# A recurrent kernel on one core: the opening's loads in another order, the cell ahead of long sums, the head's work dealt anew

## The chip, the cores and the metric

One core of a Trainium2 chip runs the kernel. Its engines are the tensor engine (PE, with its weight loads shown as PEld), the vector engine (DVE), the scalar engine (ACT), GpSimd (POOL), and SyncE (SP), whose queue issues every DMA of this kernel. The 16 DMA engines of the core serve that one queue. The metric is the time of one execution on the device in microseconds (us), as the median of several runs; lower is better.

## The reference

The kernel computes an LSTM over 512 steps for a batch of 32, hidden size 512, and adds the result to its input, all in float32:

```python
xW = einsum('ntd,dg->ntg', x, Wx) + b        # (32, 512, 2048)
def step((h, c), xw_t):
    a = xw_t + h @ Wh                         # four gates of 512
    i, f, o = sigmoid(a[:, :512]), sigmoid(a[:, 512:1024]), sigmoid(a[:, 1024:1536])
    g = tanh(a[:, 1536:])
    c = f * c + i * g
    h = o * tanh(c)
    return (h, c), h
out = x + hs                                  # hs: the h of all steps
```

## The kernel before, in words

**Two kinds of matmul.** Each of the 512 steps needs the recurrent product `h @ Wh` (`h_part`, L254), which depends on the step before, and the projection `x @ Wx` of its own x. The projection of steps 20 to 499 is not made step by step. It is made for 15 groups of 32 steps with a scheme of Strassen's kind: 26 products per group, each as seven small products `r` (L541), between left factors made of sums of rows of x (`pair_sum` L486 to L492, `make_sum` L455, held in `xs0`, `xs1` and `ubuf`) and right factors made of sums of weight blocks. Each product ends in a C buffer (`evacuate`, L595 to L611), and the C buffers are combined with long sums of 128x1024 (`w_op`, L402) and stored to DRAM (`xwd`), from where each step's four gate rows are read back three steps ahead (`load_xw`). This work is called the stream. It is counted in quarters: four to a small product, 28 to a product, 728 to a group. The first group's stream lies in the head, steps 0 to 19. Later groups are dealt evenly over the steps.

**Opening and head.** Before step 0, PE makes plain projections for steps 0 to 4 (`KEPT`) and for step 13 (`FIRST`), L190. The projections of steps 5 to 12 and 14 to 19 are made inside the head steps, as `HEAD_PLAINS` deals them; those of steps 11 and later wait in `xw` or in DRAM (`kept`). `HEAD_STREAM` says how many quarters each head step takes. In the same time DVE makes the sums of weight blocks: 8 to 25 by `v_sum` (L711 for whole tiles, L714 for three pieces), in rooms that are reused in the order of `V_ROOMS`, and SP stores them to `vdram` (L718, two DMAs of 768 and 128 KB each), from where each row of the stream loads its right factors into a ring of three (`vring`, `load_v`). A room is overwritten only when its store has landed. Eight of the factors are raw weight blocks (`v_raw`, `V_DIRECT`). `jobs[t]` says what of this falls into step t, behind which projection.

**The order inside a head step.** `h_part(t)` is issued first, then the stores and loads of the step's top on SP. What follows is a list of chunks: a plain projection, or some quarters of the stream. From a given step on the first chunk is 24 quarters. In a stream chunk the program issues in this order: loads of right factors, u sums, `evacuate`, pair sums that are due (`row_jobs`), more u sums, long sums while the planner's account `room["dve"]` of free DVE time allows it, bias copies into the banks (`seed_banks`, L574; eleven products start from a combination of bias rows), the matmuls, and, behind the first chunk, the cell (`cell`, L269 to L288). Every engine runs its own instructions in the order of issue, so an instruction that waits holds all behind it on its engine; SP too.

**Buffers.** C buffers come from a pool `free_c`: eight at first, six more from step 9. One of them (number 9, `spare`) lies in the third slot of `xnat` and is taken out when that slot is needed for x: for the third chunk of eight steps at step 10 or later, and for the last chunk near the end. `xs1`, the room of the fourth pair row, lies over the first two blocks of the raw weights, so that its load for the first group (`load_row(0, 3)`) must come behind the last plain projection of the head.

**The end.** The last 12 steps' projections are plain again (`plain_part`, L199), with weights that are loaded once more by `late_loads` at the steps of `LATE`.

Of the kernel before, what the change touches and what calls it, by code (L numbers as in the profile page):

```python
# [39 lines left out]
SPLIT = END + 2  # L40
LATE = (453, 455, 457, 463, 465, 467, 469)

FIRST = 13
HEAD_PLAINS = ((14, 15), (16, 17), (18, 19), (5,), (6,), (11, 12), (7,), (8,), (9,), (10,))
HEAD_STREAM = (0, 0, 0, 0, 0, 8, 40, 52, 56, 56, 56, 60, 60, 60, 60, 60, 56, 44, 32, 28)
V_DIRECT = (2, 3, 7, 8, 15, 17, 21, 24)

U_SUMS = {
# [56 lines left out]
def kernel(  # L105
# [53 lines left out]
    def load_x(c, a=0, b=TC):  # L159
        nc.sync.dma_start(  # L160
            out=xnat[:, xslot(c), a:b].rearrange("p t q b -> p (t q b)"), in_=x[c][:, a * P : b * P]
        )
# [318 lines left out]
    def pair_sum(g, qs):  # L481
        z = pairs_at(min(PLACES[g % 2][q] for q in qs), len(qs))
        a21, a11, a12, a22, s1, s2, s3, s4 = (z[:, :, n] for n in range(8))
        i = group(g).summed[qs[0]]
        if i == 0:
            add(s1, a21, a22)  # L486
        elif i == 1:
            sub(s2, s1, a11)
        elif i == 2:
            sub(s3, a11, a21)  # L490
        else:
            sub(s4, a12, s2)  # L492
        for q in qs:
            group(g).summed[q] += 1
        room["dve"] -= cost_dve(256 * len(qs))

    row_loads = [(R * g + p, g, q) for g in range(1, NG) for p, q in ((-10, 0), (-9.5, 1), (-2.5, 2), (3.5, 3))]
    row_sums = [(1.5, 0, (2,))] * 4 + [(7.5, 0, (3,))] * 4
    for g in range(1, NG):
        row_sums += [(R * g - 7.5, g, (0, 1))] * 4 + [(R * g - 0.5, g, (2,))] * 4 + [(R * g + 5.5, g, (3,))] * 4  # L500
    row_sums.sort()
# [84 lines left out]
            make_u(max(items[i][1] for i in range(max(0, last - 7), last + 1)))  # L586

    def evacuate():
        for slot, r in finished:
            gr, s = group(slot // R), slot % R  # L590
            xb = xbank[slot % 5]
            if r == 5:
                gr.have[s, "c"] = take(free_c)
                t = buf_of(gr.have[s, "c"])
                nc.scalar.copy(t[:, 0:4:3], xb.rearrange("p (n c) -> p n c", n=2))  # L595
                continue
            if r in (1, 6):
                continue
            t = buf_of(gr.have[s, "c"])
            if r == 2:  # L600
                add(t[:, 0], bbank[:, slot % 2 * HW : (slot % 2 + 1) * HW], t[:, 0])  # L601
                room["dve"] -= cost_dve(256)
            elif r == 3:
                nc.scalar.copy(t[:, 1], xb[:, 0:HW])
                add(t[:, 1], xb[:, HW:W], t[:, 1])
                room["dve"] -= cost_dve(256)
            elif r == 7:
                add(t[:, 3], xb[:, 0:HW], t[:, 3])
                room["dve"] -= cost_dve(256)
            else:  # L610
                nc.scalar.copy(t[:, 2], xb[:, 0:HW])  # L611
                gr.have[s] = gr.have.pop((s, "c"))
                ready(gr, s)
        finished.clear()
# [127 lines left out]
    def v_raw(s):  # L742
        v_store(s, v_parts(V_OF[s]))
# [59 lines left out]
    with tc.manual_schedule():  # L803
# [4 lines left out]
        for c in range(4):  # L808
# [2 lines left out]
                out=r1[:, 4 * ko : 4 * ko + 4, 2 * ki : 2 * ki + 2].rearrange("p j s c -> p j (s c)"),  # L811
                in_=wx[c].rearrange("p (j c) -> p j c", j=NJ),
            )
        load_x(0, 5, 8)
        for j in range(NJ):
            nc.sync.dma_start(
                out=bias_full[j * B : (j + 1) * B], in_=bias[j : j + 1].to_broadcast([B, W])
# [2 lines left out]
        for k in range(NJ):  # L820
            nc.sync.dma_start(
                out=wh_sb[:, k].rearrange("p j c -> p (j c)"), in_=wh[:, k * NJ * W : (k + 1) * NJ * W]
            )
        load_x(1)
        load_x(2, 0, 4)
        for n in range(6):
            for j in range(NJ):
# [25 lines left out]
        sums = lambda *ids: [lambda i=i: v_sum(i) for i in ids]  # L853
        jobs[0] = sums(13, 14, 15, 16)
        jobs[1] = sums(17, 18, 19, 20)
        jobs[2] = sums(21, 22) + [lambda: pair_sum(0, (0, 1))] * 4 + sums(23)
        jobs[3] = [lambda: u_ahead(8)] + sums(24) + [lambda: load_v_to(1)]
        jobs[4] = sums(25) + [lambda: load_v_to(2), lambda: u_ahead(24)]
        jobs[5] = [early_seeds, lambda: u_ahead(28)] + [lambda s=s: v_raw(s) for s in V_DIRECT[4:]]
        jobs[8] = [late_seeds]  # L860
        jobs[9] = [lambda: free_c.extend(range(NC + 1, NC + 7))]
        chunk_2 = []

        HEAD_STEPS = STREAM0
# [9 lines left out]
        for t in range(T):  # L874
# [8 lines left out]
                load_x(c)  # L883
            if t == 3 * TC + 2:
                free_c.append(NC)
            if t >= SPLIT - 16 and not last_x and NC in free_c:
                free_c.remove(NC)
                last_x.append(t)
            if last_x and t == last_x[0] + 3:
# [10 lines left out]
            if t == 1:  # L900
                load_row(0, 0)
                load_row(0, 1)
            if t == 5:
                load_seeds(((4, 1), (5, 0)))
                load_row(0, 2)
            if t == 7:
                load_seeds(((1, 0), (3, 2), (2, 3)))
            if t == 10:
                load_row(0, 3)
            if PARKED <= t + 3 < HEAD + NG * GS:  # L910
                load_xw(t + 3)

            if t < HEAD_STEPS:
                plain = [("plain", p) for p in (HEAD_PLAINS[t] if t < len(HEAD_PLAINS) else ())]
                left = HEAD_STREAM[t]
                chunks = []
                if t > 5:
                    chunks.append(("stream", 24))
                    left -= chunks[0][1]
                while plain or left:  # L920
# [9 lines left out]
                for i, (kind, m) in enumerate(chunks):  # L930
# [12 lines left out]
                    else:  # L943
# [2 lines left out]
                        if i == 0:  # L946
                            room["dve"] = min(room["dve"], 1000.0) + PLAIN
                        evacuate()
                        if i < 2:
                            row_jobs(2)  # L950
                        u_ahead(m + 24)
                        while wqueue and (room["dve"] > 800 or len(free_c) < 2):
                            w_op()
                        seed_banks(m)
                        emit_matmuls(m)
                        room["dve"] += m * PROD / 4
                        if i == 0:
                            cell(t)
                            room["dve"] -= 2500.0
                if t + 1 in SEEDED:  # L960
                    seed_step(t + 1)
                if t >= 5:
# [100 lines left out]
```

## Time and profile before

| what | value |
|---|---|
| median of 3 runs | 3102.54 us (3098.99 to 3103.0) |
| profiled execution | 3098.27 us |
| its span | 3096.5 us |
| instructions | 108375 |
| PE busy | 3064.6 us (99%) |
| DVE busy | 2350.9 us (76%) |
| ACT busy | 1472.6 us (48%) |
| bytes moved by DMA | 756.94 MB, mean 244 GB/s |

A row of the timeline reads: start in us from the span's beginning, length in us of the merged pieces, engine, line of the kernel, operation, tile written and tiles read, shape, number of instructions; in square brackets the idle time of that engine just before and what ended it. "SPq" is the issue of a DMA by SP, not the transfer. A row "DMA to landing" gives the time from issue to landing, least, median and most, of the DMAs that one line issued in a given stretch. A row of a table by stretch has the stretch, its length, busy time and instructions of PE, PEld, DVE, ACT and POOL, the clock granted to PE as a share of full speed, the share of the 16 DMA engines' time, and GB/s. Starts of matmuls are measured, their ends are modelled, so distances between starts are used for their cost.

### The profile page before, as it was taken

To read this page: it belongs to the slowest core of one execution; us is meant where nothing else is said; L and a number is where in the kernel's file an instruction comes from. 1 tells how busy PE (TensorE), PEld (TensorE's weight loads), DVE (VectorE), ACT (ScalarE), POOL (GpSimd) and SP (SyncE) were. 2 spreads that over 40 slices of the span, in tenths; PEclk is the share of its full clock that TensorE was granted. 3 is DMA by queue.
4 is the path that set the end of the run, shared out by engine and by line. 5 is a ranking of instruction groups with operands and counts; after the bars stand their busy time and mean duration, and the time that the engine had idled before them with its cause. 6 is when DMAs were issued, how large, how long until landed. Compare 5 with 4: busy or idle time off the path is not lost.

```text
span 3096.5 us, 108375 instructions
## 1 busy us (share of the span) xinstructions
PE 3064.6 (99%) x43600; PEld 1651.6 (53%) x43600; DVE 2350.9 (76%) x6381; ACT 1472.6 (48%) x5528; POOL 237.9 (8%) x508
## 2 busy tenths in 40 slices
PE   8999999999999999999999999999999999999998
PEld 5644555555555555555555555555555555555575
DVE  7588778787877878778787787878778787787644
ACT  1344445445444454544445454454545545454444
POOL 0000000000000000000000000000000000000110
PEclk9999999999999999999999999999999999999999
DMA  9788878787787777778777787777878777778530
GB/s 359 244 283 279 279 233 271 237 262 244 245 270 239 255 248 244 262 242 268 234 258 259 228 271 241 260 248 242 266 241 265 238 251 259 247 260 257 175 92 21
DMA packets 320151, 756.94 MB, mean 244 GB/s; under 512 B 50976, under 2 KB 102432, under 8 KB 319136
## 3 DMA queue, kind: packets, MB, share of 16 engines
q1 hardware_dynamic: 319648, 750.00, 73.8%
q8 instruction: 344, 5.64, 0.8%
q14 instruction: 159, 1.30, 0.1%
HBM read 568.13 MB, written 184.81 MB: 243 GB/s over the span
## 4 chain that ended last, share of the span: by engine, by line
PE 94%; DVE 2%; DMA 1%; ACT 1%; issue 0%; SPq 0%; DVEq 0%; ACTq 0%
PE gbank L254 53%; PE xbank L541 32%; PE bbank L541 5%; PE xbank L254 2%; PE xbank L199 1%; PE gbank L190 0%; DMA vdram<-xs 0%; DVE cbuf L402 0%; DVE r L402 0%; DVE prod L273 0%; DVE s L274 0%; DMA vdram<-vring 0%; DVE vring L714 0%; DMA seeds_own<-in_L_cond_b_dram 0%; DMA r<-in_x_grouped_dram 0%
## 5 line engine op out<-in xcount | busy, mean ns | idle before, releaser
L254 PE MATMUL gbank<-wh_sb,ht 128*32 128x512 f32 (+1 forms) x16288 | 1778.6, 575 | 6.4 <-DVE ht L280 3.6
L254 PEld LDWEIGHTS gbank<-wh_sb,ht 128*32 128x32 f32 x16288 | 606.0, 110 | 833.2 <-issue 703.3
L269 ACT ACTIVATE s<-gbank 128x128 f32<-128x128 f32 x976 | 273.6, 280 | 1233.4 <-PE gbank L254 1232.8
L541 PE MATMUL xbank<-vring,ubuf 128*32 128x256 f32 (+1 forms) x13632 | 854.2, 369 | 2.3 <-ACT xnat L595 2.3
L541 PEld LDWEIGHTS xbank<-vring,ubuf 128*32 128x32 f32 x13632 | 527.9, 110 | 296.1 <-issue 134.5
L273 DVE TENSOR_TENSOR prod<-s 128x128 f32<-128x128 f32 x1024 | 293.9, 287 | 479.7 <-ACT s L270 475.5
L288 POOL TENSOR_TENSOR oc<-xnat,ht 128x128 f32<-128x128 f32 x504 | 237.7, 472 | 2820.8 <-DVE ht L280 1343.9
L276 ACT ACTIVATE tanh_c<-s 128x64 f32<-128x64 f32 x1024 | 262.6, 257 | 252.4 <-DVE s L274 250.8
L280 DVE STREAM_TRANSPOSE ht<-hbuf 128x64 f32<-128x64 f32 x1022 | 250.9, 245 | 75.2 <-DVE hbuf L278 0.7
L676 ACT COPY gbank<-xw 128x512 f32<-128x512 f32 x459 | 276.0, 601 | 0.0
L274 DVE TENSOR_TENSOR s<-prod 128x64 f32<-128x64 f32 x1024 | 230.3, 225 | 35.2
L278 DVE TENSOR_TENSOR hbuf<-o,tanh_c 128x64 f32<-128x64 f32 x1024 | 211.7, 207 | 30.7 <-ACT tanh_c L276 30.3
L270 ACT ACTIVATE s<-gbank 128x64 f32<-128x64 f32 x976 | 224.4, 230 | 0.0
L541 PE MATMUL xbank<-vring,xs 128*32 128x256 f32 (+1 forms) x3216 | 209.7, 358 | 4.5 <-ACT xbank L574 4.5
L541 PE MATMUL xbank<-vring,r 128*32 128x256 f32 (+1 forms) x3216 | 208.3, 357 | 0.0
L541 PE MATMUL bbank<-vring,ubuf 128*32 128x256 f32 (+1 forms) x2608 | 185.4, 342 | 2.2 <-DVE cbuf L601 2.2
L541 PEld LDWEIGHTS xbank<-vring,r 128*32 128x32 f32 x3216 | 122.5, 110 | 80.6 <-issue 47.5
L541 PEld LDWEIGHTS xbank<-vring,xs 128*32 128x32 f32 x3216 | 124.5, 110 | 65.6 <-issue 24.6
L271 ACT ACTIVATE o<-gbank 128x128 f32<-128x128 f32 (+1 forms) x509 | 153.5, 302 | 0.0
L402 DVE TENSOR_TENSOR cbuf<-cbuf 128x1024 f32<-128x1024 f32 x122 | 148.8, 1223 | 0.4
L541 PEld LDWEIGHTS bbank<-vring,ubuf 128*32 128x32 f32 x2608 | 101.6, 110 | 69.7 <-issue 38.6
L402 DVE TENSOR_TENSOR r<-r,cbuf 128x1024 f32<-128x1024 f32 x106 | 128.5, 1215 | 0.5
(138 smaller groups left out, 2562.2 us busy)
## 6 DMA issues: line engine op xcount, KB each, us to landing
vring<-vdram SPq DMA_DIRECT2D x311, 896.0 KB, 5.5
xw<-xwd SPq DMA_DIRECT2D x1920, 64.0 KB, 4.2
xwd<-cbuf SPq DMA_DIRECT2D x117, 512.0 KB, 4.6
xwd<-r SPq DMA_DIRECT2D x105, 512.0 KB, 4.2
out_dram<-oc SPq DMA_DIRECT2D x255, 128.0 KB, 4.0
xnat<-in_x_dram SPq DMA_DIRECT2D x63, 512.0 KB, 6.0
xs<-in_x_grouped_dram SPq DMA_DIRECT2D x45, 512.0 KB, 4.6
vring<-vdram SPq DMA_DIRECT2D x35, 512.0 KB, 4.9
```

The source lines that it names most:

```text
L254: nc.tensor.matmul(dst[j * B : (j + 1) * B], state["ht"][:, k], m, start=False, stop=True, skip_group_check=True)
L269: nc.scalar.activation(s[:, u, 0:2], g[:, n_, 0:2], AF.Sigmoid)
L270: nc.scalar.activation(s[:, u, 2], g[:, n_, 3], AF.Tanh)
L273: nc.vector.tensor_mul(prod[:, u], s[:, u, 0:2], s[:, u, 2:4])
L274: add(nxt[:, u, 3], prod[:, u, 0], prod[:, u, 1])
L276: nc.scalar.activation(tanh_c[:, HALVES[u]], nxt[:, u, 3], AF.Tanh)
L278: nc.vector.tensor_mul(hbuf[:, HALVES[u]], o[:, u], tanh_c[:, HALVES[u]])
L280: nc.vector.transpose(ht[:, 2 * u : 2 * u + 2].rearrange("p q b -> p (q b)"), hbuf[:, HALVES[u]])
L288: (nc.gpsimd if t < T - 8 else nc.vector).tensor_add(oc[:, tt % 2], x_of(t), ht)
L402: op(c_of(dst), c_of(src), c_of(bb))
L541: nc.tensor.matmul(dst[j * B : (j + 1) * B, cols], left_of(gr, s, r)[:, j * B : (j + 1) * B], vring[:, row % 3, RIGHT[r], cols], start=sta ...
L676: nc.scalar.copy(bank_of(t), src)
```

## The change

- In the opening, the part of x that holds step 13 (`load_x(1, 5, 6)`, 64 KB) is loaded where x of steps 5 to 7 was (192 KB), ahead of the bias. The other parts of x of the first 16 steps follow behind the recurrent weights in three pieces.
- `HEAD_PLAINS`: projections 5 and 6 both in step 3, 11 and 12 in step 4, none in step 5; `HEAD_STREAM` differs in five steps. A first chunk of 24 quarters exists from step 5 on instead of step 6; since step 5's entry is 16, the step issues 24 and the account is squared after the head.
- `jobs`: the first two rows' pair sums go from step 2 to step 3, the late raw stores from step 5 to step 6, the sums of bias rows (`early_seeds`) from step 5 to step 4. Two bias rows are loaded at step 3 instead of 5. The last pair row of the first group is loaded in step 9 behind the projection instead of at the top of step 10, and its sums come at position 9.3 rows instead of 7.5.
- In the first chunk of a head step, pair sums and u sums are left to the next chunk, and long sums run only while the planner's account is above 2200 or no buffer is free. Pair sums go up to four to a later chunk. In a step without projections, jobs run behind the cell.
- `evacuate` runs long sums first when the pool is too small for what it has to take.
- The last chunk of x takes its slot up to 24 steps sooner (`SPLIT - 40` instead of `SPLIT - 16`).

```diff
-HEAD_PLAINS = ((14, 15), (16, 17), (18, 19), (5,), (6,), (11, 12), (7,), (8,), (9,), (10,))
-HEAD_STREAM = (0, 0, 0, 0, 0, 8, 40, 52, 56, 56, 56, 60, 60, 60, 60, 60, 56, 44, 32, 28)
+HEAD_PLAINS = ((14, 15), (16, 17), (18, 19), (5, 6), (11, 12), (), (7,), (8,), (9,), (10,))
+HEAD_STREAM = (0, 0, 0, 0, 0, 16, 40, 48, 56, 56, 60, 60, 60, 60, 60, 56, 52, 44, 32, 28)
...
-    row_sums = [(1.5, 0, (2,))] * 4 + [(7.5, 0, (3,))] * 4
+    row_sums = [(1.5, 0, (2,))] * 4 + [(9.3, 0, (3,))] * 4
...
     def evacuate():
+        while wqueue and len(free_c) < sum(r == 5 for _, r in finished):
+            w_op()
...
-        load_x(0, 5, 8)
+        load_x(1, 5, 6)
...
-        load_x(1)
+        load_x(1, 6, 8)
+        load_x(0, 5, 8)
+        load_x(1, 0, 5)
         load_x(2, 0, 4)
...
-        jobs[2] = sums(21, 22) + [lambda: pair_sum(0, (0, 1))] * 4 + sums(23)
-        jobs[3] = [lambda: u_ahead(8)] + sums(24) + [lambda: load_v_to(1)]
-        jobs[4] = sums(25) + [lambda: load_v_to(2), lambda: u_ahead(24)]
-        jobs[5] = [early_seeds, lambda: u_ahead(28)] + [lambda s=s: v_raw(s) for s in V_DIRECT[4:]]
+        jobs[2] = sums(21, 22, 23)
+        jobs[3] = [lambda: pair_sum(0, (0, 1))] * 4 + [lambda: u_ahead(8)] + sums(24) + [lambda: load_v_to(1)]
+        jobs[4] = sums(25) + [lambda: u_ahead(24), early_seeds]
+        jobs[6] = [lambda s=s: v_raw(s) for s in V_DIRECT[4:]]
         jobs[8] = [late_seeds]
-        jobs[9] = [lambda: free_c.extend(range(NC + 1, NC + 7))]
+        jobs[9] = [lambda: load_row(0, 3), lambda: free_c.extend(range(NC + 1, NC + 7))]
...
-            if t >= SPLIT - 16 and not last_x and NC in free_c:
+            if t >= SPLIT - 40 and not last_x and NC in free_c:
...
+            if t == 3:
+                load_seeds(((4, 1), (5, 0)))
             if t == 5:
-                load_seeds(((4, 1), (5, 0)))
                 load_row(0, 2)
...
-            if t == 10:
-                load_row(0, 3)
...
-                if t > 5:
+                if t > 4:
                     chunks.append(("stream", 24))
...
                         evacuate()
-                        if i < 2:
-                            row_jobs(2)
-                        u_ahead(m + 24)
-                        while wqueue and (room["dve"] > 800 or len(free_c) < 2):
-                            w_op()
+                        if i == 0:
+                            while wqueue and (room["dve"] > 2200 or len(free_c) < 1):
+                                w_op()
+                        else:
+                            row_jobs(4)
+                            u_ahead(m + 24)
+                            while wqueue and (room["dve"] > 800 or len(free_c) < 2):
+                                w_op()
                         seed_banks(m)
                         emit_matmuls(m)
                         room["dve"] += m * PROD / 4
                         if i == 0:
                             cell(t)
                             room["dve"] -= 2500.0
+                            while todo and not plains:
+                                todo.pop(0)()
+                                flush_v()
```

## The prediction

> **What bounds the kernel now.** I read the page's first part, then the table of engines by stretch, the grouped lines of the long middle, and the timeline at each idle piece of the tensor engine (PE).
>
> ```profile
> PE 3064.6 (99%) x43600; PEld 1651.6 (53%) x43600; DVE 2350.9 (76%) x6381; ACT 1472.6 (48%) x5528; POOL 237.9 (8%) x508
> L254 PE MATMUL gbank<-wh_sb,ht 128*32 128x512 f32 x13852 | 1577.4, 592 | 0.1
> ```
>
> PE is busy 99% of the span, and from 250 to 2800 us it waits 0.1 us ahead of the recurrent products (L254) and for nothing else. The change removes and adds no matmul. So it can only move PE's idle time at the two ends, and the time PE runs at half clock behind an idle piece. This is where that time stands:
>
> ```profile
> 23.17 2.85 PE L190 MATMUL xbank<-r,xnat 128*32 128x256 f32 x48
> 32.18 5.36 PE L190 MATMUL xbank<-r,xnat 128*32 128x256 f32 x64 [6.16 <-DMA xnat<-in_x_dram]
> 76.14 3.64 PE L254 MATMUL xbank<-wh_sb,ht 128*32 128x512 f32 x32 [0.68 <-DVE ht L280]
> 101.16 1.07 PE L541 MATMUL xbank<-vring,ubuf 128*32 128x256 f32 x16 [2.35 <-ACT xnat L595]
> 158.12 1.70 PE L541 MATMUL xbank<-vring,xs 128*32 128x256 f32 x16 [4.53 <-ACT xbank L574]
> 221.61 0.64 PE L541 MATMUL bbank<-vring,ubuf 128*32 128x256 f32 x8 [2.20 <-DVE cbuf L601]
> 224.74 3.64 PE L254 MATMUL gbank<-wh_sb,ht 128*32 128x512 f32 x32 [0.33 <-ACT gbank L676]
> 240.76 3.64 PE L254 MATMUL gbank<-wh_sb,ht 128*32 128x512 f32 x32 [0.75 <-ACT gbank L676]
> 248.67 3.64 PE L254 MATMUL gbank<-wh_sb,ht 128*32 128x512 f32 x32 [1.24 <-ACT gbank L676]
> 2900.31 0.41 PE L199 MATMUL xbank<-r,seeds_own 128*32 128x256 f32 x2 [1.19 <-DMA r<-in_L_cond_Wx_dram]
> ```
> ```profile
> 30.00:40.00 10.00, 7.82 (x92) 4.25 (x96) 4.94 (x8) 0.00 (x0) 0.00 (x0) 0.72 1.02 368
> 57.50:62.50 5.00, 5.00 (x68) 2.88 (x63) 4.96 (x8) 2.39 (x8) 0.00 (x0) 1.00 0.87 254
> 62.50:90.00 27.50, 26.82 (x404) 17.41 (x397) 21.83 (x50) 7.81 (x30) 3.78 (x4) 1.00 1.03 381
> 100.00:110.00 10.00, 8.84 (x148) 6.45 (x152) 5.08 (x16) 4.47 (x15) 0.46 (x1) 1.00 1.02 359
> 150.00:160.00 10.00, 5.47 (x89) 3.87 (x84) 4.83 (x15) 3.26 (x13) 0.45 (x1) 0.92 0.52 166
> 160.00:170.00 10.00, 10.00 (x136) 4.51 (x132) 7.40 (x19) 4.59 (x15) 0.46 (x1) 0.91 0.91 304
> ```
>
> In the stretches the columns behind the length are PE, weight loads, vector engine (DVE), ACT, POOL, then granted clock, DMA share and GB/s. Two things carry everything below: the idle of 4.53 us is followed by a clock of 0.92 and 0.91, that is 10 x (0.08 + 0.09) = 1.7 us more lost, and the DMA engines are full (share 1.02 and 1.03) from 30 to 90 us but for a dip at 60.
>
> **The change part by part.**
>
> *x of step 13 first.* The last block of the opening ends at 23.17 + 2.85 = 26.02; step 13's projection then waits until x lands, behind the recurrent weights.
>
> ```profile
> 37.30 3.67 PE L254 MATMUL gbank<-wh_sb,ht 128*32 128x512 f32 x32
> 40.73 3.71 PE L190 MATMUL xbank<-r,xnat 128*32 128x256 f32 x64
> 44.19 3.71 PE L190 MATMUL bbank<-r,xnat 128*32 128x256 f32 x64
> 47.64 3.69 PE L254 MATMUL gbank<-wh_sb,ht 128*32 128x512 f32 x32
> DMA to landing us min/median/max: 10.1/11.3/12.5
> ```
>
> By the distances between starts a recurrent product costs 3.43, a projected step 3.46, a step with two of them 10.34. With 64 KB of x ahead of the bias instead of 192 KB, the projection runs from 26.02 to 29.48, and step 0 begins there instead of at 37.30: 7.82 us sooner. The recurrent weights do not hold it: the last quarter was issued at 18.3 and landed 12.5 later (row of those loads), at 30.8, and is used in the last quarter of the product, at 32.05. The two added x loads cost an SP issue each with no waiter near.
>
> *What then takes the place of that wait.* The DMA engines were already full, so stores of the weight sums (`v_sum`, L711/L714) land when they did. A sum may only overwrite a room whose older store has landed:
>
> ```profile
> 32.96 1.29 DVE L714 TENSOR_TENSOR ubuf<-cbuf 128x768 f32<-128x768 f32 x2
> 63.33 1.73 SPq L718 DMA_DIRECT2D vdram<-xs  x2
> DMA to landing us min/median/max: 8.9/9.0/9.1
> 72.48 0.96 DVE L714 TENSOR_TENSOR xs<-r,ubuf 128x768 f32<-128x768 f32 x1 [1.44 <-DMA vdram<-xs]
> 74.56 0.28 DVE L273 TENSOR_TENSOR prod<-s 128x128 f32<-128x128 f32 x1
> ```
>
> Sum 23 uses the room of sum 19 and waits for its store, 63.33 + 9.1 = 72.4, today; that is the 0.68 of PE at 76.14. It stays the last sum of step 2, ahead of step 3's cell on DVE. Sooner PE: step 3 begins at 29.48 + 3 x 10.34 = 60.50, now has two projections (5 and 6), and ends at 60.50 + 3.43 + 6.92 = 70.85. DVE is through sum 22 at about 64 (sum 12 ends at 32.96 + 1.29 = 34.25; step 13's bias add 0.7, ten sums at 2.1 and three cells at 1.8 make 61.4; rooms that come free at the DMA's pace add an estimated 3), then stands until the store lands. I let it land 0.2 sooner, at 72.2 (ends: 70.7, if the dip of 57.5 to 62.5, (381-254)/381 x 5 = 1.7 us, is filled; 72.5 as now). Sum 23 takes 74.56 - 72.48 = 2.08, the cell 76.14 - 74.56 = 1.58: step 4 starts at 75.86, PE having idled 5.0 us, and runs 1.7 longer at half clock as behind the 4.53. The nearest idle below, 2.35, kept the clock at 1.00 (row 100 to 110), so I take the price of the row nearest to 5.0; its other end is 0. The Trainium skill ("TensorE: Matmul & The Clock Gate", Part 1) says that the clock halves after one wholly idle window of about 3.4 us that runs freely, so that an idle of 5.0 holds a whole one in only some half of the phases; by that rule alone the term is 1.7 or nothing and the gain below 11.2 or 12.9, and the trace has one idle on each side and none that tells.
>
> So step 4 ends at 75.86 + 3.43 + 1.7 + 6.92 = 87.91 (projections 11 and 12), step 5's product at 91.34. There the stream of Strassen products (L541) begins; today, with exactly the same projections and products behind it, it begins at
>
> ```profile
> 93.39 1.12 PE L541 MATMUL xbank<-vring,ubuf 128*32 128x256 f32 x16
> 81.93 2.29 SPq L644 DMA_DIRECT2D vring<-vdram  x2
> DMA to landing us min/median/max: 5.7/5.7/5.8
> 94.26 3.69 PE L254 MATMUL gbank<-wh_sb,ht 128*32 128x512 f32 x32
> ```
>
> Gain there 93.39 - 91.34 = **2.05**, all that is left of 7.82 + 0.68. It can't be much more in any case: the weights of its first two rows landed at 81.93 + 1.2 + 5.8 = 88.9, behind a full DMA, and the two bias rows (256 KB each, 1.4 us at 381 GB/s) are now ahead of them: 90.3, a ceiling of 3.1 unless the store queue moves up too.
>
> *Bias rows at step 3.* Today they land late, and two engines stand for it:
>
> ```profile
> 98.71 0.69 DVE L766 TENSOR_TENSOR seeds_own<-seeds_own 128x512 f32<-128x512 f32 x1 [9.51 <-DMA seeds_own<-in_L_cond_b_dram]
> 99.48 0.59 ACT L574 COPY xbank<-seeds_own 128x512 f32<-128x512 f32 x1 [5.15 <-DVE seeds_own L766]
> 101.01 0.28 ACT L269 ACTIVATE s<-gbank 128x128 f32<-128x128 f32 x1
> 102.72 0.24 DVE L280 STREAM_TRANSPOSE ht<-hbuf 128x64 f32<-128x64 f32 x1
> ```
>
> The 2.35 at 101.16 goes: **+2.35**.
>
> *Stream dealt anew.* 16 quarters more before step 11, the total is kept; no PE time. But step 5 loses its cover: it had two projections between product and next step, now 24 quarters (0.109 each: 8 in 94.26 - 93.39), 2.6 us. After 16 of them two copies of xbank stand ahead of the cell on ACT, because the third item needs them: 1.74 + 0.59 + 1.95 (cell, 101.01 to 102.96) = 4.28. **-1.7**; ends 0 (copies not ahead) and -2.6. The raw stores of step 5 move behind projection 7 of step 6: 8 issues, 2 MB; rows 3 and 4 now go ahead of them, the late bias rows behind, needed only four steps later. Nothing.
>
> *Row 3 of x's sums.*
>
> ```profile
> 154.45 0.43 DVE L486 TENSOR_TENSOR r<-r 128x256 f32<-128x256 f32 x1 [5.95 <-DMA r<-in_x_grouped_dram]
> 155.84 0.26 ACT L276 ACTIVATE tanh_c<-s 128x64 f32<-128x64 f32 x1 [4.81 <-DVE s L274]
> ```
>
> Four sums wait for a load of step 10's top, ahead of that step's cell. Now the load goes out behind projection 10, 32 quarters (3.5 us) sooner, and the sums come 48 quarters and the cell later. **+6.2** (4.53 + 1.7).
>
> *Cell ahead of long sums.* Chunk 0 does at most some two sums of 1.2 us, no pair sums, no u sums. Idle of the late head: 2.20 + 0.33 + 0.75 + 1.24 = 4.52. The work only moves a chunk back and DVE is nearly full there:
>
> ```profile
> 162.49:212.32 49.83, 49.83 (x765) 24.49 (x761) 42.29 (x94) 25.51 (x79) 2.30 (x5) 1.00 0.95 326
> 212.32:254.51 42.19, 37.67 (x533) 16.67 (x530) 35.53 (x81) 17.41 (x61) 1.82 (x4) 1.00 0.80 253
> ```
>
> I take half, **+2.3** (ends +4.5 and -4.5).
>
> *Last x sooner; the guard in `evacuate`.* A 512 KB load and one of 16 buffers move some 30 steps ahead. The wait at 2900 is for a weight load that the change leaves: **0**; ends +1.2 and -2 (guard's sums of 1.2 us where two buffers are free).
>
> Sum: 2.05 + 2.35 - 1.7 + 6.2 + 2.3 = **11.2**. The profiled execution took 3098.27 (span 3096.5): 3087.1. The median of the runs, 3102.54, lies 4.3 above it (0.14%); on it the same sum gives 3091.3. I name the middle, 3089.
>
> **The rivals.**
> *The store queue moves up too.* No wait for sum 23: for it speaks the dip at 60, against it share 1.03 behind the dip. Gain 7.82 + 0.68 + 2.35 - 1.7 + 6.2 + 2.3 = 17.7: 3083 (middle of both bases). Chance 0.17.
> *It does little.* Step 13's wait comes back in full at step 4 (gain 0 at the stream), and the late head keeps its 4.5 us: 2.35 - 1.7 + 6.2 = 6.9, or 0.7 if row 3 is late again, since its load waits on SP for projection 10's last read of its room: 3091 to 3102 over both bases, taken at 3096. Chance 0.22.
> *DVE becomes the bound of the late head: slower.* Sums held back in chunk 0 pile up in chunk 1 ahead of the adds that free banks, as where 2.20 us was lost at 221.61. At 2.2 in each of the steps 11 to 20 it costs 22, against 8.9 gained before: 13 us slower, 3114. From seven such steps on it is slower by over 0.2%; DVE has 7.5 us to spare in steps 11 to 15 and none lost PE anything. Chance 0.08.
> The forecast itself keeps 0.53 (own range 3084 to 3096); 0.15 of this is a clock that does not drop at step 4 (gain 12.9, 3087 in the middle), which is inside that range.
>
> **How the numbers follow.** A measurement of this kernel tells about 0.2% (6.2 us) from no change: the line is 3096.3. Faster: 0.51 of the forecast, the 0.17, little of the 0.22: 0.69. Same: most of the second rival and edges: 0.21. Slower: 0.10, the 0.08 and a little for buffers. The range reaches from the first rival, 3080, to the end of the second, 3101.
>
> **What would show it.** Step 13's projection at 26 without a wait, step 0 near 29.5; a DVE wait of some 8 us for a store of `xs`, an idle of about 5 ahead of step 4's product and a clock under 1 behind it; the stream's start near 91; an idle of 1 to 2 ahead of step 6; none by L574 at 98 and none near 150; at most 2.3 from step 16 to 20. It is wrong if the store lands by 70, or if chunk 1's sums hold `bbank` in several steps.

## The result, and the profile after

The changed kernel takes 3095.93 us (median of 15 runs, 3092.77 to 3098.98), the kernel before 3101.93 us beside it (15 runs): a ratio of 0.998, with a 95% interval from 0.9972 to 0.9988. It is 6.0 us faster where 11.2 were forecast; 3095.93 lies inside the range, but 7 us above the number named. The profiled execution took 3095.93 us, its span is 3094.2.

The timeline of PE in the changed kernel, the rows that answer to the idle pieces shown of before. Lines moved by two: L597, L603, L613, L678 and L716 are the former L595, L601, L611, L676 and L714. The rows at 29.04, 255.85 and 3085.90 show only a part of their product, and serve for their starts alone.

```profile
29.04 3.26 PE L254 MATMUL gbank<-wh_sb,ht 128*32 128x512 f32 x28
73.60 5.03 PE L254 MATMUL xbank<-wh_sb,ht 128*32 128x512 f32 x32 [2.94 <-DVE ht L280]
90.06 1.07 PE L541 MATMUL xbank<-vring,ubuf 128*32 128x256 f32 x16 [1.01 <-DMA vring<-vdram]
94.77 3.64 PE L254 MATMUL gbank<-wh_sb,ht 128*32 128x512 f32 x32 [1.70 <-DVE ht L280]
212.63 1.93 PE L541 MATMUL xbank<-vring,ubuf 128*32 128x256 f32 x32 [1.74 <-ACT r L613]
242.51 5.34 PE L254 MATMUL gbank<-wh_sb,ht 128*32 128x512 f32 x32 [4.21 <-ACT gbank L678]
250.05 3.64 PE L254 MATMUL gbank<-wh_sb,ht 128*32 128x512 f32 x32 [0.68 <-DVE hbuf L278]
255.85 0.64 PE L254 MATMUL gbank<-wh_sb,ht 128*32 128x512 f32 x4
3085.90 0.64 PE L254 MATMUL gbank<-wh_sb,ht 128*32 128x256 f32 x8 [0.79 <-DVE ht L280]
```

Step 0 starts at 29.04, the stall of step 10 near 150 and the wait at 101 are gone. In their place stands a new idle of 4.21 us ahead of step 20, and the product behind it takes 5.34 instead of 3.64 us. The table by stretch shows why: the clock, the first figure behind the busy times of the five engines, is 0.54 there (columns as in the prediction).

```profile
73.00:76.50 3.50, 2.90 (x16) 0.79 (x20) 3.23 (x9) 1.25 (x3) 0.81 (x1) 0.51 1.06 406
150.00:160.00 10.00, 9.76 (x148) 5.33 (x144) 7.91 (x19) 4.60 (x15) 0.46 (x1) 1.00 0.99 382
243.50:247.20 3.70, 3.70 (x24) 0.89 (x20) 0.85 (x1) 0.00 (x0) 0.00 (x0) 0.54 0.89 263
```

DVE and ACT from their timelines, first the sum that waits for its store, then what stands around the new idle:

```profile
69.93 0.96 DVE L716 TENSOR_TENSOR xs<-r,ubuf 128x768 f32<-128x768 f32 x1 [6.46 <-DMA vdram<-xs]
...
231.39 1.21 DVE L402 TENSOR_TENSOR r<-cbuf,r 128x1024 f32<-128x1024 f32 x1
...
234.91 1.22 DVE L402 TENSOR_TENSOR r<-r,cbuf 128x1024 f32<-128x1024 f32 x1
238.01 0.24 DVE L280 STREAM_TRANSPOSE ht<-hbuf 128x64 f32<-128x64 f32 x1
240.87 0.58 ACT L597 COPY cbuf<-xbank 128x512 f32<-128x512 f32 x1 [2.93 <-DMA xwd<-cbuf]
241.35 0.60 ACT L574 COPY xbank<-seeds_own 128x512 f32<-128x512 f32 x1
241.87 0.59 ACT L678 COPY gbank<-xw 128x512 f32<-128x512 f32 x1
```

The h of step 19 was ready at 238.25 (238.01 + 0.24). PE waited for `gbank`, the bank that a copy on ACT (`seed_step`, L678) fills with the projection of step 20. That copy stood in ACT's queue behind an evacuation (L597) that waited 2.93 us: it writes a C buffer whose last store had not landed, for the program gives a buffer back to the pool when its store is issued.

Where the time went, between the two profiled executions. Step 22 starts at 260.31 before and at 255.85 after, with equally many quarters of the stream done. Step 11 starts at 162.49 and 154.39, with 16 quarters (1.74 us) more done after.

| piece | forecast | from the traces |
|---|---|---|
| start of the stream | +2.05 | 93.39 - 90.06 = +3.3 |
| bias rows sooner | +2.35 | +2.35 (no idle at 101) |
| cover of step 5 | -1.7 | -1.70 |
| row 3 of x | +6.2 | +6.2 (no idle, no half clock) |
| all of it at step 11 | +8.9 | 162.49 - 154.39 + 1.74 = +9.8 |
| late head, step 11 to 22 | +2.3 | 4.46 - 9.84 = -5.4 |
| steady part, step 22 to the last | 0 | -2.1 |
| sum | +11.2 | +2.3 |

The medians show 6.0 where these executions show 2.3, since the profiled execution of before lies 3.7 below its median and that of after on it. The table is of one execution each; what a row is worth in others shows in the experiments.

### The profile page after: what moved, and what is told of

It reads as the page before. It is cut to its first block, busy times and chain, and to the rows that moved or that the text cites. A ratio compares the mean times of both kernels' runs of the same rounds, so it can differ in the third digit from the quotient of the medians.

```text
span 3094.2 us, 108367 instructions
## 1 busy us (share of the span) xinstructions
PE 3067.0 (99%) x43600; PEld 1639.2 (53%) x43600; DVE 2350.1 (76%) x6381; ACT 1472.8 (48%) x5528; POOL 236.4 (8%) x508
## 4 chain that ended last, share of the span: by engine, by line
PE 94%; DVE 2%; DMA 1%; ACT 1%; issue 0%; SPq 0%; DVEq 0%; ACTq 0%
PE gbank L254 53%; PE xbank L541 31%; PE bbank L541 5%; PE xbank L254 2%; PE xbank L199 1%; PE gbank L190 0%; DVE prod L273 0%; DVE cbuf L402 0%; DVE s L274 0%; DMA vring<-vdram 0%; DMA vdram<-xs 0%; DVE hbuf L278 0%; DVE ht L280 0%; DMA vdram<-vring 0%; ACT s L269 0%
## 5 line engine op out<-in xcount | busy, mean ns | idle before, releaser
L276 ACT ACTIVATE tanh_c<-s 128x64 f32<-128x64 f32 x1024 | 262.3, 256 | 258.7 <-DVE s L274 254.1
L280 DVE STREAM_TRANSPOSE ht<-hbuf 128x64 f32<-128x64 f32 x1022 | 250.9, 246 | 77.2 <-DVE hbuf L278 3.4
L678 ACT COPY gbank<-xw 128x512 f32<-128x512 f32 x459 | 276.0, 601 | 0.3
L402 DVE TENSOR_TENSOR r<-r,cbuf 128x1024 f32<-128x1024 f32 x112 | 136.0, 1219 | 0.2
```

The lines of the kernel that those rows point to most:

```text
L276: nc.scalar.activation(tanh_c[:, HALVES[u]], nxt[:, u, 3], AF.Tanh)
L280: nc.vector.transpose(ht[:, 2 * u : 2 * u + 2].rearrange("p q b -> p (q b)"), hbuf[:, HALVES[u]])
L402: op(c_of(dst), c_of(src), c_of(bb))
L678: nc.scalar.copy(bank_of(t), src)
```

## The experiments

All times below are medians beside runs of the kernel before on the same chip (3101.7 to 3102.2 us). Two numbers serve for comparison: the time, and the length of the late head from the start of step 11 to that of step 22, which is 101.46 us in the changed kernel and 97.82 in the kernel before, or 96.08 for equal work.

**The surplus of 8 quarters.**

```diff
-HEAD_STREAM = (0, 0, 0, 0, 0, 16, 40, 48, 56, 56, 60, 60, 60, 60, 60, 56, 52, 44, 32, 28)
+HEAD_STREAM = (0, 0, 0, 0, 0, 16, 40, 48, 56, 56, 60, 60, 60, 60, 60, 56, 52, 44, 24, 28)
```

> The changed kernel with one number altered: step 18 gets 24 quarters of stream instead of 32, so the head ends with 728 quarters issued instead of 736, and the seed copies of gbank for step 20 come on ACT ahead of the evacuation copy that waited 2.93 us for the store of its own buffer. Theory (a buffer is given back when its store is issued, not when it has landed; the copy into it stands in ACT's queue ahead of the seeds that step 20 needs): the idle of 4.21 us at 242.5 and the 1.7 us of half clock behind it shrink to under 1 us together, 3 to 6 us faster than the changed kernel, a ratio to the kernel before of about 0.9965. Rival (DVE has more work in steps 16 to 20 than fits, so the same time is lost one step on): the idle moves to another step of the late head, no difference to the changed kernel, 0.998.

Measured: 3092.75 us, ratio 0.9968 (0.9957 to 0.998). The late head takes 96.50. The idle ahead of step 20 is 1.17 and the clock stays whole; the evacuation copy still waits 3.13 us for its store, but now behind the seed copy, where nobody waits for it. That fits the theory, though the deal changed too, so the next runs separate the copy from it.

**A store that reads elsewhere, first try.**

```diff
-                in_=buf_of(buf).rearrange(...),
+                in_=(cbuf[:, 6] if now[0] == 19 else buf_of(buf)).rearrange(...),
```

> The changed kernel, where the weight stores of step 19 read the bias rows in place of the summed weights (same bytes, same places in DRAM, wrong values: part of the streamed products is computed from wrong weights). The buffers of those sums are then not read by their stores. Everything else, order of work on every engine too, is as in the changed kernel. Theory (ACT waits for the store of its own buffer): the 2.93 us wait of the evacuation copy on the stores goes, the idle of 4.21 us at 242.5 falls to below 1.5 us and the clock stays whole, 3 to 5 us faster than the changed kernel, about 0.9968 of the kernel before. Rival (the copy would come late anyway, behind DVE's four long sums at 231 to 236): the idle stays above 3 us and the time at 0.998.

Measured: 3097.14 us, 0.9981 (0.9972 to 0.999), late head 100.69, idle of 3.08 ahead of step 20. The edit met nothing: followed through the program, step 19 issues no such store, and the two that matter are issued by step 18. The run is the changed kernel once more and serves as its repeat.

**The same, at the right step.**

```diff
+                in_=wh_sb[:, 0, 0:2] if now[0] == 18 else buf_of(buf).rearrange(...),
```

> The changed kernel, where the stores that the program issues in step 18 (two of group 0's summed products) read the recurrent weights in SBUF in place of the sums: same bytes, same places in DRAM, same order of all work, but wrong values for two blocks of the projected x. No C buffer is then read by these stores. Theory (the evacuation copy at 240.9 waits on ACT only for the store of its own buffer to land): that wait of 2.93 us goes, the idle of 4.21 us ahead of step 20 falls below 1.5 us, the half clock behind it goes, 3 to 5 us faster than the changed kernel, about 0.9965 to 0.997 of the kernel before. Rival (the copy stands behind work of PE or DVE that is as late as the store): the idle stays at 3 us or more, 0.998.

Measured: 3092.43 us, 0.997 (0.9959 to 0.9981), late head 96.74. Its timeline of ACT and PE (L599, L680 are L597, L678 here):

```profile
240.11 0.59 ACT L599 COPY cbuf<-xbank 128x512 f32<-128x512 f32 x1
241.10 0.60 ACT L680 COPY gbank<-xw 128x512 f32<-128x512 f32 x1
241.76 3.64 PE L254 MATMUL gbank<-wh_sb,ht 128*32 128x512 f32 x32 [1.34 <-ACT gbank L680]
```

The copy waits for nothing, the idle is 1.34 and step 20's product takes its normal 3.64. The order of work on every engine is the old one; only what the two stores read differs, and with it the time at which the buffer is free. That is worth 4.7 us (3097.14 - 3092.43), or 3.5 against the first median of the changed kernel. The wait for the store is the cause of this loss.

**The seed copies ahead of the last evacuation.**

```diff
                             room["dve"] = min(room["dve"], 1000.0) + PLAIN
+                        elif i == len(chunks) - 1 and t + 1 in SEEDED:
+                            seed_step(t + 1)
                         evacuate()
```

> The changed kernel with one thing moved: in steps 11 to 20 the seed copies of the next step go out on ACT ahead of the evacuation of the last chunk, not behind it. All stores and buffers stay as they are. Theory (what cost the late head is the place of the seed copy in ACT's queue, behind a copy that waits for a store): the evacuation copy still waits 2 to 3 us for the store, but the idle ahead of step 20 falls below 1.5 us and the half clock goes, 3 to 5 us faster than the changed kernel, about 0.9967 of the kernel before. Rival (PE needs what the waiting copy frees anyway, so the idle only moves behind step 20's product): 2 us or more of idle inside step 20, 0.998.

Measured: 3092.13 us, 0.9968 (0.9956 to 0.9981), late head 96.33.

```profile
239.88 0.59 ACT L678 COPY gbank<-xw 128x512 f32<-128x512 f32 x1 [0.16 <-issue]
241.60 0.59 ACT L597 COPY cbuf<-xbank 128x512 f32<-128x512 f32 x1 [0.83 <-DMA xwd<-cbuf]
240.52 3.64 PE L254 MATMUL gbank<-wh_sb,ht 128*32 128x512 f32 x32 [0.85 <-ACT gbank L678]
```

The evacuation still waits, 0.83 and not the 2 to 3 us expected, and PE no longer depends on it. So the loss took two things together: a buffer given back before its store has landed, and a copy that PE needs placed behind it.

**The old rule for chunks, from step 11 on.**

```diff
-                        if i == 0:
+                        if i == 0 and t < 11:
                             while wqueue and (room["dve"] > 2200 or len(free_c) < 1):
                                 w_op()
                         else:
-                            row_jobs(4)
+                            if i < 2 or t < 11:
+                                row_jobs(4 if t < 11 else 2)
```

> The changed kernel, with the old rule for chunks (two row jobs in each of the chunks 0 and 1, u sums and long sums ahead of the cell) from step 11 on; everything before step 11 and the new deal of stream as in the changed kernel. Theory A (the cell ahead of long sums gained what was forecast, about 2 us, and the loss at step 20 comes from the surplus of stream quarters): the idle of steps 11 to 19 grows by some 2 us and the one at 242.5 stays, 0.9985 to 0.999 of the kernel before. Theory B (the rule itself pushes sums late and makes the 4.21 us): the idle at 242.5 goes, those of steps 16 to 19 come back at about 4.5 us in all, and the time is 2 to 4 us under the changed kernel's, 0.997.

Measured: 3093.14 us, 0.9971 (0.9959 to 0.9982), late head 96.74. Theory B held. The rows of PE with idle from step 16 on:

```profile
222.67 0.64 PE L541 MATMUL xbank<-vring,ubuf 128*32 128x256 f32 x8 [1.76 <-DMA vring<-vdram]
231.30 3.64 PE L254 MATMUL gbank<-wh_sb,ht 128*32 128x512 f32 x32 [1.10 <-DVE cbuf L603]
238.81 3.64 PE L254 MATMUL gbank<-wh_sb,ht 128*32 128x512 f32 x32 [0.85 <-ACT gbank L678]
244.65 3.64 PE L254 MATMUL gbank<-wh_sb,ht 128*32 128x512 f32 x32 [0.68 <-DVE hbuf L278]
```

Idle of 4.39 in all, as the 4.52 of before, and from 205 to 262 us no copy of ACT waits for a store. Where the new rule is freed of its side effect (late head 96.33 with the seeds ahead) it is no better than the old one (96.08 before, for equal work); with seeds ahead and rooms exchanged, below, it takes 96.19 under the new rule and 93.80 under the old. By these single executions the cell ahead of long sums gains nothing here. That the sums then stand ahead of another cell is the likely reason, but no run separates it.

**x of step 13 alone, on the kernel before.**

```diff
-        load_x(0, 5, 8)
+        load_x(1, 5, 6)
...
-        load_x(1)
+        load_x(1, 6, 8)
+        load_x(0, 5, 8)
+        load_x(1, 0, 5)
```

> The kernel before with one part of the change alone: x of step 13 is loaded ahead of the bias, x of steps 5 to 12 behind the recurrent weights. Theory (the gain is handed back at the store that sum 23 waits for, and at the weights of the stream's first rows): step 0 starts at 29 to 30.5 instead of 37.3, PE idles 3 to 5 us ahead of step 4 and runs at half clock for up to 1.7 us, the stream starts at 90 to 92 instead of 93.4; 0 to 3 us faster than the kernel before, 0.999 to 1.000. Rival (stores and loads move up with it): the stream starts near 86 and the time falls by 7 us or more, 0.9977.

Measured: 3100.69 us, a ratio of 1.0 (0.9991 to 1.0009). Its timelines of DVE and PE, and a row of its table by stretch:

```profile
72.59 0.96 DVE L714 TENSOR_TENSOR xs<-r,ubuf 128x768 f32<-128x768 f32 x1 [4.39 <-DMA vdram<-xs]
76.26 6.38 PE L254 MATMUL xbank<-wh_sb,ht 128*32 128x512 f32 x32 [8.07 <-DVE ht L280]
96.27 1.12 PE L541 MATMUL xbank<-vring,ubuf 128*32 128x256 f32 x16
```
```profile
71.60:81.84 10.24, 5.58 (x28) 1.38 (x32) 8.04 (x16) 1.00 (x3) 1.21 (x1) 0.50 1.05 396
```

Sum 23 waits for its store to 72.59, as it did before the edit (72.48), and PE idles 8.07 us, more than the 3 to 5 expected. The clock is at half for 10.24 us, of which 5.58 lie behind the restart (81.84 - 76.26) and cost half of that, 2.8. That is the whole of the distance by which the stream starts later, 96.27 against the 93.39 of before, as step 4 starts when it did (76.26 and 76.14). Seven microseconds won at step 0 are worth nothing while the store lands when it did.

**Row 3 of x alone, on the kernel before.**

```diff
-        jobs[9] = [lambda: free_c.extend(range(NC + 1, NC + 7))]
+        jobs[9] = [lambda: load_row(0, 3), lambda: free_c.extend(range(NC + 1, NC + 7))]
...
-            if t == 10:
-                load_row(0, 3)
```

> The kernel before with row 3 of x loaded as the second-last job of step 9 instead of at the top of step 10; the place of the four sums that use it is left as it was. Theory (the stall of step 10 was the distance between load and sums alone): the idle of 4.53 us at 158.1 and the half clock of 1.7 us behind it go, 6 us faster, 0.998. Rival (the load of row 3 waits on SP for projection 10's last read of its room, so an earlier issue brings little): at least 2 us of the idle stay and the time is 0 to 3 us below the kernel before, 0.9995.

Measured: 3095.92 us, 0.998 (0.9972 to 0.9989): 5.8 us faster, as much as the whole change. Its timeline of PE, and its table by stretch:

```profile
102.85 1.94 PE L541 MATMUL xbank<-vring,ubuf 128*32 128x256 f32 x16 [3.95 <-ACT xnat L595]
219.83 0.64 PE L541 MATMUL bbank<-vring,ubuf 128*32 128x256 f32 x8 [2.20 <-DVE cbuf L601]
```
```profile
101.40:108.20 6.80, 5.35 (x52) 2.58 (x56) 3.53 (x11) 4.04 (x13) 0.46 (x1) 0.50 1.05 355
150.00:160.00 10.00, 10.00 (x156) 6.53 (x148) 7.48 (x21) 4.41 (x15) 0.46 (x1) 1.00 0.86 291
220.90:224.20 3.30, 3.30 (x37) 1.62 (x32) 3.14 (x6) 1.45 (x3) 0.00 (x0) 0.50 0.94 357
```

PE has no idle piece from 150 to 160. The other rows show code that this edit leaves as before, in another execution: the wait for the bias rows is 3.95 instead of 2.35, with half a clock behind it until 108.2, which costs (108.2 - 102.85) x 0.5 = 2.7 us more, and the idle of 2.20 now drags half a clock too. So the profiled execution of before was a lucky one. The bias rows can cost more than the 2.35 read from it, and less: with x of step 13 alone, where the stream starts later, PE waits 0.43 us at that place. What they are worth to the median no run measured.

**The rooms of sums 23 and 24 exchanged.**

```diff
-V_ROOMS = (5, 0, 1, 2, 6, 3, 4, 0, 1, 2, 3, 7, 0, 6, 1, 7, 5, 2)
+V_ROOMS = (5, 0, 1, 2, 6, 3, 4, 0, 1, 2, 3, 7, 0, 6, 1, 5, 7, 2)
```

> The changed kernel with the rooms of two weight sums exchanged: sum 23 writes into the room of an older sum, sum 24 into the one of sum 19, so the cell of step 3 no longer stands behind a sum that waits for a store. Theory (the gain of the earlier step 13 is held at two places, first by that store and then by the full DMA engines): step 4 starts near 70.5 to 71 instead of 73.6 with no idle above 1 us and no half clock, but the stream still cannot start before its weights land at 89 to 90, so 0 to 1 us faster than the changed kernel. Rival (the wait for the store is the only bound): the stream starts near 86 to 87 and the time falls by 3 to 4.5 us, to 0.9968 of the kernel before.

Measured: 3094.72 us, 0.9977 (0.9968 to 0.9987). Its timeline of PE, and a row of its table by stretch:

```profile
70.97 3.69 PE L254 MATMUL xbank<-wh_sb,ht 128*32 128x512 f32 x32
88.60 1.93 PE L541 MATMUL xbank<-vring,ubuf 128*32 128x256 f32 x16 [3.60 <-DMA vring<-vdram]
```
```profile
87.80:91.20 3.40, 2.60 (x28) 1.41 (x32) 0.00 (x0) 0.58 (x1) 0.00 (x0) 0.50 1.05 404
```

Step 4 starts at 70.97 without idle, and the stream waits for its weights to 88.60 with half a clock behind: the second hold that the prediction named, at a DMA share of 1.05. It is 1.2 us faster than the changed kernel, inside the scatter of both.

**Combinations.** Old rule, rooms, bias rows at step 4 and 16 quarters in step 5:

> The changed kernel with the old rule for chunks from step 11 on, the rooms of sums 23 and 24 exchanged, the two bias rows loaded at step 4 (behind the weights of the stream's first rows) instead of step 3, and 16 instead of 24 quarters in the first chunk of step 5. Theory (each of the four places costs what its idle shows): step 4 near 71 without idle, stream start 1 to 2 us sooner than where only the rooms are exchanged, idle ahead of step 6 below 0.6 instead of 1.70 us, no idle above 2 us behind it; 2 to 4 us faster than with the old rule alone, about 0.996 of the kernel before. Rival (the bias rows, now later, are late again, and step 5 loses its cover): an idle of 2 us or more ahead of the third item of the stream or of step 6, no faster than the old rule alone, 0.997.

Measured: 3099.63 us, 0.9991 (0.9983 to 1.0). The rival held. Its timelines of DVE and PE:

```profile
91.84 0.69 DVE L768 TENSOR_TENSOR seeds_own<-seeds_own 128x512 f32<-128x512 f32 x1 [10.99 <-DMA seeds_own<-in_L_cond_b_dram]
95.13 6.23 PE L254 MATMUL gbank<-wh_sb,ht 128*32 128x512 f32 x32 [3.86 <-DVE ht L280]
```

DVE stood 10.99 us for the bias rows, and step 6 started after 3.86 us of idle at half clock. The stream started hardly sooner for their new place: at 88.51, against 88.60 with the rooms alone (and 89.79 to 91.53 in the three kernels below with the rooms exchanged; single executions). Behind the deal that is now 8 quarters short, the stream stalls 3.05 us in step 8.

Seeds ahead, rooms and 24 quarters in step 18:

> The changed kernel with three edits: the seed copies ahead of the last evacuation, the rooms of sums 23 and 24 exchanged, and 24 quarters in step 18. Theory (gains at separate places add): step 4 near 71 without idle, stream start near 88 to 89, idle from step 16 to 21 about 3 us in all, 4 to 6 us faster than the changed kernel, about 0.9962 of the kernel before. Rival (the places share one limit, the DMA engines or the buffers): no faster than the best single edit, 0.997.

Measured: 3091.87 us, 0.997 (0.9958 to 0.9981), no better than the best single edits: what the rooms give at step 4 (71.43) is lost again, with an idle of 6.08 for the weights ahead of the stream at 91.53.

Seeds ahead, rooms, and 16 quarters in step 5:

> As the run before, but the 8 quarters are taken from the first chunk of step 5 (16 instead of 24), which is what the deal's entry says, and step 18 keeps its 32; the bias rows are loaded at step 3. Theory (the idle of 1.70 us ahead of step 6 comes from two copies of xbank that the third item needs and that stand ahead of the cell): that idle falls below 0.6 us, 1 us faster than the run before. Rival (the shift of the whole deal by 8 quarters puts other long sums ahead of a cell in steps 11 to 20): idle of over 2 us at a place where the changed kernel has none, and no faster.

Measured: 3096.76 us, 0.9983 (0.9974 to 0.9992). Step 6 has no idle, but PE stands still in steps 8 and 18 (its timelines of DVE and PE, then its table by stretch):

```profile
129.48 1.09 DVE L455 TENSOR_TENSOR ubuf<-xs,ubuf 128x896 f32<-128x896 f32 x1
130.67 2.37 PE L541 MATMUL xbank<-vring,ubuf 128*32 128x256 f32 x40 [3.04 <-issue]
233.57 1.23 DVE L455 TENSOR_TENSOR ubuf<-xs,ubuf 128x896 f32<-128x896 f32 x1
234.90 1.88 PE L541 MATMUL xbank<-vring,ubuf 128*32 128x256 f32 x16 [2.18 <-issue]
```
```profile
130.70:134.00 3.30, 3.30 (x60) 2.33 (x64) 1.94 (x4) 1.50 (x4) 0.00 (x0) 1.00 0.28 88
235.00:238.40 3.40, 3.40 (x28) 1.63 (x31) 3.37 (x6) 0.59 (x1) 0.00 (x0) 0.50 0.97 318
```

The profile names no releaser for these two ("issue"). But the products read `ubuf`, and both times PE goes on 0.10 us behind the end of a u sum of DVE that writes it (129.48 + 1.09 = 130.57, and 233.57 + 1.23 = 234.80); the stall of the run above in step 8 ends in the same way (134.14 and 134.24). So the stream waits there for its left factors, which DVE makes late. In step 8 of both runs DVE was busy with sums of bias rows just before. That the 24 quarters of step 5 cost 1.70 us of cover and are still the better choice is shown only for these two deals.

Old rule, rooms and seeds ahead:

> The changed kernel with the old rule for chunks from step 11 on, the rooms of sums 23 and 24 exchanged and the seed copies ahead of the last evacuation. Theory (under the old rule no evacuation waits for a store, so the order of the seed copies only takes the small idles of 0.7 to 1.1 us): step 4 near 71, idle from step 16 to 21 at 2 to 4.5 us, 0 to 2 us faster than with the old rule alone, 0.9965 of the kernel before. Rival (the seed copies now delay the evacuation that frees a bank): idle from step 16 to 21 above 5 us, 0.9975.

Measured: 3090.86 us (3090.18 to 3093.76), 0.9968 (0.9956 to 0.998): the lowest median of all, 5.1 us below the changed kernel. Ahead of it the stream waits 5.00 us for its weights and starts at 90.41. The late head takes 93.80, with one idle above 1 us left:

```profile
223.88 0.64 PE L541 MATMUL xbank<-vring,ubuf 128*32 128x256 f32 x8 [1.53 <-DMA vring<-vdram]
238.18 3.62 PE L254 MATMUL gbank<-wh_sb,ht 128*32 128x512 f32 x32
```

The intervals don't tell it apart from the seeds ahead alone (3092.13).

## Why the prediction was right and wrong

The mechanism was right up to step 11, a term behind it had the wrong sign, and one was left out.

**x of step 13 first: right.** The chain named (step 0 sooner, sum 23 behind the store of sum 19, idle ahead of step 4 with half a clock, then the loads of the ring as the ceiling) is what the traces show. In the changed kernel's own execution sum 23 went on at 69.93 and not 72.2, below even the bound of 70.7, so step 4 had 2.94 of idle instead of 5.0. The prediction had named a store that lands by 70 as a sign of being wrong, and here it did; it was issued at 61.84, 1.5 us sooner than before. The stream still started only at 90.06 (forecast 91.34), when its weights had landed. This is one execution and luck in part. In five other kernels with the same opening (the first surplus run, the repeat, the old rule, the store elsewhere and the seeds ahead) sum 23 goes on between 70.10 and 73.62, step 4 starts between 73.76 and 77.29 and the stream between 89.30 and 92.52. In the repeat it starts at 91.28 but stands 1.97 us more behind its first 16 products; with that counted in, the six give a mean of 91.6, which is a gain of 1.8 against the forecast's 2.05. The rival "the store queue moves up too" falls with the rooms: without the store's wait the stream stands at its own weights. In the five kernels with the rooms it starts between 88.51 and 91.53, about the ceiling of 90.3; whether the bias rows' 1.4 us belong into that ceiling these single executions don't tell.

**Bias rows, cover of step 5, row 3: right.** 2.35, -1.70 and 6.2 against the same numbers in the forecast; row 3 alone measured 5.8 us. The cost of the bias rows was read from one execution; in two others it was 3.95 with half a clock behind it, and 0.43.

**"Cell ahead of long sums: I take half, +2.3": wrong.** This is the step that failed. The late head lost 5.4 us (4.6 in the repeat, 4.3 with the rooms), about or beyond the lower end of the -4.5 to +4.5 that was allowed, and the idle from step 16 to 20, at most 2.3 us by the forecast, was 6.57. The working looked at DVE time only, and put the danger in sums ahead of the adds that free banks. The danger was elsewhere: on ACT, in a wait for a DMA, through the pool of C buffers. Of the loss, 3.5 to 4.7 us is shown by the store that reads elsewhere and 3.8 by the seeds ahead. That nothing was gained beside it shows in 96.33 against 96.08. Without that wait the change is 9.3 us faster than the kernel before (the store elsewhere) or 10.0 (the seeds ahead), close to the 11.2 of the forecast. The row that warned stood in the profile of before, on ACT, where the prediction did not look:

```profile
248.03 0.58 ACT L676 COPY gbank<-xw 128x512 f32<-128x512 f32 x1
249.86 0.59 ACT L595 COPY cbuf<-xbank 128x512 f32<-128x512 f32 x1 [1.25 <-DMA xwd<-cbuf]
```

An evacuation waited 1.25 us for the store of its own buffer already then; it stood behind the seed copy, where PE did not need it.

**The steady part: left out.** From step 22 to the last step the changed kernel is 2.1 us slower (255.85 to 3085.90, against 260.31 to 3088.27). It doesn't look like scatter: the kernel before takes 2828.0 us there, the two that change only x of step 13 or row 3 in it 2827.8 and 2827.4, and the ten kernels built on the changed one 2828.7 to 2830.8 (itself 2830.0). The timeline of DVE shows the place of the largest part, first in the changed kernel, then in the kernel before, both in step 85:

```profile
632.12 0.23 DVE L278 TENSOR_TENSOR hbuf<-o,tanh_c 128x64 f32<-128x64 f32 x1
632.81 0.24 DVE L280 STREAM_TRANSPOSE ht<-hbuf 128x64 f32<-128x64 f32 x1 [0.46 <-DVE hbuf L278]
```
```profile
636.58 0.23 DVE L278 TENSOR_TENSOR hbuf<-o,tanh_c 128x64 f32<-128x64 f32 x1
636.91 0.24 DVE L280 STREAM_TRANSPOSE ht<-hbuf 128x64 f32<-128x64 f32 x1
```

Between two instructions of DVE's own pass 0.36 us more, in a step where no slack is left, and the next product starts 0.33 later. Such a hole stands in seven steps of the changed kernel (85, 103, 203, 221, 403, 448, 479) and in one of before (248).

The work is not another: from step 27 on both programs issue the same instructions in the same order, but for the load of the last x and the numbers of the buffers. What differs is the place. Count an engine's instructions through the trace from 0, its waits on semaphores included. Between 262 and 3085 us of the 14 kept traces, each of the 72 holes ahead of a transpose (L280) that follows a wait stands where the transpose has a number that leaves 63 on division by 128, and every such transpose with such a number has one. On ACT a tanh (L276) that follows a wait starts 0.34 to 0.36 us behind the start of that wait at such a number, and at most 0.06 at any other; in the changed kernel this falls on steps 143, 284, 293 and 399 among others, which take 0.24 or 0.25 longer than before. The steps in which such a place of DVE or ACT falls differently in the two kernels make 2.2 us of net loss, which is all of the 2.1. The change has DVE issue 7197 instructions in place of 7204 and ACT 7366 in place of 7371, so the places move to other steps. That more of them fell on steps without slack is chance; why they cost time isn't shown.

**The rest.** The last x and the guard cost nothing that the traces show; the waits at the end are 0.41, 0.87 and 1.29 (0.41, 1.19 and 1.30 before). "It does little" came nearest in its time (3096), but not in its mechanism: the opening gave what the forecast said, and the late head took it back. That row 3 alone gives 5.8 of the 6.0 us is no sign that the rest did nothing; gains and the loss cancel.

## What to carry to other kernels

When work is moved behind a critical instruction, follow the buffers and not only the engine's time: list what each engine has queued in front of the next thing that the bottleneck needs, and which of these waits for a transfer. A pool that takes a buffer back when its store is issued hides such a wait, and a copy for the bottleneck belongs in front of it. A gain at the start of a chain is worth only what the next fixed time (here a store, then a load, on full DMA engines) leaves of it.

## What the runs showed of the hardware

The granted clock falls in spells of 3.41, 6.83 or 10.24 us, but the length of the idle doesn't decide alone. Up to step 22, in the kept traces, every idle piece of 3.3 us and more had such a spell with it and none under 2 us had one; of the ten between 2.1 and 3.1 us five had it. 2.20 us left the clock at 1.00 in the kernel before (the row below, its table by stretch) and halved it in the kernel with row 3 alone, at the same place; 2.18 halved it and 3.04 did not, in one execution of one kernel; 2.94 halved it in the changed kernel. (Idle is counted from the modelled end of a matmul.) The Trainium skill ("TensorE: Matmul & The Clock Gate", Part 1) has the clock halve after at least one idle window of about 3.4 us, and its windows run freely. The lengths of the spells agree with such windows; that a whole window has to be idle these rows don't bear out, since idle of about two thirds of one was enough at times. So an idle piece of 2 to 3 us has a price of 0 or up to 1.7 us (half of 3.41) that one profile can't tell, and a profiled execution can be lucky by several microseconds (3.7 here, against its median).

```profile
221.60:225.00 3.40, 3.06 (x52) 1.61 (x56) 3.40 (x6) 1.75 (x4) 0.00 (x0) 1.00 0.87 283
```
